# A two-layer graph-attention kernel on one core: the start of step 0, the rows of flags of step 1, the guard and the code behind it are moved

## The chip, the core and the metric

The kernel runs on one core of a Trainium2 chip. The core has five engines that run their own instruction streams: TensorE (PE, with its weight loads shown as PEld), VectorE (DVE), ScalarE (ACT), GpSimd (POOL) and SyncE (SP). An engine takes its instructions in order; one that needs another engine's result waits for a semaphore. The metric is the time of one execution on the device in microseconds (us). Before the change, three runs gave 3081.44, 3081.27 and 3081.38 us (median 3081.38).

## The reference

There are 64 graphs of 256 nodes with 512 features. Two layers of masked attention run over each graph; all is float32.

```python
def _layernorm(x): return (x - mean(x)) / sqrt(var(x) + 1e-5)

# layer 0: 4 heads of 64, keys masked by adj
h = maximum(_layernorm(x), 0)
sim = where(adj, (h @ Wq) (h @ Wk)^T / 8, -max_float)      # per head
x = x + softmax(sim) (h @ Wv) @ Wo + bo
# layer 1: 8 heads of 64, keys masked by adj | eye
h = maximum(_layernorm(x), 0)
g = _layernorm(h) * gamma + beta
scores = where(adj | eye, q k^T / 8, -1e9)                 # q, k, v = split(g @ w_qkv.T)
x = x + softmax(scores) v @ w_out.T + b_out
```

A row of `adj` without any edge makes the first softmax uniform. The kernel handles this by a flag per row: `any_of` is the maximum of a row of `adj`, and q and the mask are multiplied by the flag.

## The kernel before

**Two paths.** `fast_path` (L317) computes the softmax without subtracting a maximum, which holds as long as no sum of exponentials leaves a range. It collects the largest sums and inverse sums in `extremes`. When it has ended, a guard (L1486 to L1494) reduces `extremes` to one number, compares it with a limit and loads the answer into a register of every engine. At L1495 every engine branches: with the answer "safe" it jumps over the code of `general_path` (L25), which would compute everything again with a maximum, to the common end. With the inputs of this case the jump is always taken; the general path is never run, but its code lies between the branch and the end on every engine.

**Steps.** The fast path takes the graphs in 32 steps of two. A projection of a step is seven products of half-size blocks (`SET`, a Strassen-like scheme), which is why lines such as L898 (q and k), L945 and L979 (values) and L995 (output) come in sets of seven with evacuations from PSUM between them. The first and last steps and layer 0 of steps 0 and 1 have forms of their own.

**The order of the work is written out by hand.** `at(period, place, function)` puts each piece at a place on a common line of time; the pieces are sorted by place and issued in that order, so the place decides the order on PE, DVE, ACT and POOL (not the moment). DMA issues of SP follow the same list. Several pieces have their own place for step 0 and step 1.

**Names that the change and the prediction touch.**

- `norm0` (L662): statistics of one tile t of 128 rows (DVE, L643 and L644), variance plus epsilon (DVE, L672), its power -1/2 (POOL, L673). `first_scale` (L681): the negative mean times it (`mr`, DVE, L684), then the scaling of the tile (ACT, L685). Step 0 has four tiles: t = 0, 1 are graph 0, t = 2, 3 are graph 1.
- `first_turn` (L787) transposes a tile by PE (L794); `first_fill` (L798) copies a graph's transposed tiles with a ReLU from PSUM to `hT`, two channel blocks by ACT (L805) and two by DVE (L803). `first_qk` (L808) is a projection of q and k of one graph and one half (PE, L816), evacuated by DVE (L823) and ACT (L824).
- `neighbours` (L579) computes `any_of` by DVE (L585). `neighbours_rows` (L604) spreads the flags into a 128 x 128 tile each (`rows`, L608), by POOL for step 0 and by DVE for step 1. `neighbours_turn` (L610) turns them by PE (L614) and ACT copies them to `ne` (L619). `adjacency_transpose` turns the adjacency by PE (L551).
- The softmax sums: `key_halves` (POOL, L1086), `turn_keys` (DVE, L1092), `key_quarters` (DVE, L1099), `turn_sums` (DVE, L1152), `key_sums` (DVE, L1160 to L1164). `mask_scores` is DVE L1074, `exponentials` ACT L1079.
- `weight_block` turns the last weight matrix by PE (L496) and copies it by ACT (L498). Its four calls lie between the products of step 1's projection.
- PSUM has four banks for products, which `mm_tile` hands out in turn; a product waits until the bank's last reader has finished.
- At the end, `combine` runs the last seven products (PE, L995), and `accumulate` adds each to the result (DVE, L853 to L866). `store_block` stores the four blocks of the output (L1009, L1012). `hint_end` (L1443) loads a zero into a register and tells an engine where the branch will go, for PE and for DVE.

Of the kernel before, what the change touches and what calls it, by code (L numbers as in the profile page):

```python
# [8 lines left out]
FP = mybir.dt.float32  # L9
# [3 lines left out]
AF = mybir.ActivationFunctionType  # L13
# [11 lines left out]
def general_path(  # L25
# [18 lines left out]
    P = 128  # L44
    B, N, D = x.shape
    DH = 64
    G = 2
    NIC = N // P
    NT = G * NIC
    T = G * N  # L50
# [88 lines left out]
    def transposed(h, name, evacuate):  # L139
        hT = act.tile([P, NC, T], FP, name=name)  # L140
        for c in range(NC):
            ph = ps_mm.tile([P, T], FP, name="mm")
            for t in range(NT):
                nc.tensor.transpose(ph[:, t * P:(t + 1) * P], h[:, t, c * P:(c + 1) * P], ident)
            evacuate(hT[:, c, :], ph, c)
        return hT

    def project(hT, w, inner, lyr):

        pairs = inner // P  # L150
        qT = act.tile([P, pairs, T], FP, name=f"qT{lyr}")
        kT = act.tile([P, pairs, T], FP, name=f"kT{lyr}")
        v = act.tile([P, NT, inner], FP, name=f"v{lyr}")
        for pr in range(pairs):
            for k, dst in ((0, qT), (1, kT)):
                pp = ps_mm.tile([P, T], FP, name="mm")
                for c in range(NC):
                    nc.tensor.matmul(
                        pp, w(c, k)[:, pr * P:(pr + 1) * P], hT[:, c, :],
                        start=(c == 0), stop=(c == NC - 1),  # L160
                    )
                nc.scalar.copy(dst[:, pr, :], pp)
        for t in range(NT):
            pv = ps_mm.tile([P, T], FP, name="mm")
            for c in range(NC):
                nc.tensor.matmul(
                    pv[:, :inner], hT[:, c, t * P:(t + 1) * P], w(c, 2),
                    start=(c == 0), stop=(c == NC - 1),
                )
            nc.scalar.copy(v[:, t, :], pv[:, :inner])  # L170
        return qT, kT, v

    def probs(qT, kT, neg, g, pr):

        sc = [ps_sc.tile([P, NIC, N], FP, name="sc") for _ in range(2)]
        for ic in range(NIC):
            for e in range(2):
                rows = slice(e * DH, (e + 1) * DH)
                i0 = g * N + ic * P
                nc.tensor.matmul(  # L180
                    sc[e][:, ic, :], qT[rows, pr, i0:i0 + P], kT[rows, pr, g * N:(g + 1) * N],
                    start=True, stop=True,
                )
        pm = sm.tile([P, 2, NIC, N], FP, name="pm")
        st = stat.tile([P, 3, 2, NIC], FP, name="st")
        for e in range(2):
            for ic in range(NIC):

                nc.vector.tensor_tensor_reduce(
                    out=pm[:, e, ic, :], in0=sc[e][:, ic, :], in1=neg[:, g * NIC + ic, :],  # L190
                    scale=-SCALE, scalar=SMAX, op0=ALU.add, op1=ALU.min,
                    accum_out=st[:, 0, e, ic:ic + 1],
                )
                nc.scalar.activation(
                    pm[:, e, ic, :], pm[:, e, ic, :], AF.Exp,
                    bias=st[:, 0, e, ic:ic + 1], scale=-1.0,
                    accum_out=st[:, 1, e, ic:ic + 1],
                )
            nc.vector.reciprocal(st[:, 2, e, :], st[:, 1, e, :])
            for ic in range(NIC):  # L200
                nc.vector.tensor_scalar(
                    pm[:, e, ic, :], pm[:, e, ic, :], st[:, 2, e, ic:ic + 1], None, op0=ALU.mult
                )
        return pm

    def weigh(pm, v, oT, g, pr):

        pT = sm.tile([P, 2, NIC, N], FP, name="pT")
        for e in range(2):
            pp = ps_pt.tile([P, NIC, N], FP, name="pt")  # L210
            for jc in range(NIC):
                for ic in range(NIC):
                    nc.tensor.transpose(
                        pp[:, jc, ic * P:(ic + 1) * P], pm[:, e, ic, jc * P:(jc + 1) * P], ident
                    )
            nc.vector.tensor_copy(pT[:, e], pp)
        po = ps_mm.tile([P, T], FP, name="mm")
# [22 lines left out]

    def combine(oT, w, pairs, res):
        for t in range(NT):
            po = ps_mm.tile([P, T], FP, name="mm")
# [74 lines left out]
def fast_path(  # L318
# [14 lines left out]
    out: bass.AP,  # L333
    ident: bass.AP,
    extremes: bass.AP,
    likely: bass.AP,
):

    nc = tc.nc
# [264 lines left out]
    def neighbours_rows(s):  # L604
        rows = S[s]["rows"] = sm.tile([P, NT, P], BF, name="rows", tag="u", bufs=1)
        for t in range(NT):
            eng = nc.gpsimd if s == 0 else nc.vector
            eng.tensor_scalar(rows[:, t, :], identb, 0.0, S[s]["any"][:, t:t + 1], op0=ALU.mult, op1=ALU.add)  # L608

    def neighbours_turn(s):  # L610
        rows = S[s].pop("rows")
# [596 lines left out]
    def at(period, place, fn, *args):  # L1208
        events.append((period * (PERIOD if period >= 0 else FIRST) + place, len(events), fn, args))
# [93 lines left out]
    for s in range(NSTEP):  # L1303
# [10 lines left out]
        else:  # L1314
            at(p - 1, 4.9, adjacency_pack, s)
        for t in range(NT):
            at(p, (0.5 + 0.4 * t, (1.6995, 1.6996, 2.0295, 2.0296)[t], -6.3 + 0.01 * t)[s] if s < 3 else (0.95, 1.05, 1.2, 1.35)[t], norm0, s, t)
            if s == 0:
                at(p, 0.95 + 0.4 * t, first_scale, t)
            else:  # L1320
                at(p, (2.375 + 0.001 * t, (-5.8, -5.799, -5.6, -5.599)[t])[s - 1] if s < 3 else 1.6 + 0.001 * t, scale_row, s, t)
            if not by_tensor(s, 0):
                at(p, AT_X - 0.00035 + 0.00001 * t if s > 2 else (2.6, 2.601, 2.72, 2.721)[t], turn_blocks, s, 0, t)
        if not by_tensor(s, 0):
            at(p, AT_X - 0.00031 if s > 2 else 3.0, move_blocks, s)
        for g in range(G):
            if s < 3:
                at(p, (1.8, 2.7, -5.8)[s] + 0.001 * g, neighbours, s, g)
            else:
                at(p - 1, AT_Q0 - 0.0009, neighbours, s, g)  # L1330
        if s < 2:
            at(p, (2.9, 2.72)[s], neighbours_rows, s)
            at(p, (3.45, 3.59)[s], neighbours_turn, s)
        else:
            at(p, -4.99 if s == 2 else 0.05, neighbours_line, s)
            at(p, -4.98 if s == 2 else 0.051, neighbours_spread, s)
# [97 lines left out]


    at(NSTEP - 2, LAST_QK + 4.1 + 2 / 7, lambda: hint_end(mybir.EngineType.PE))
    at(NSTEP - 2, LAST_QK + 4.1 + 5 / 7, lambda: hint_end(mybir.EngineType.DVE))
    at(NSTEP - 2, LAST_QK + 3.5, nc.vector.memset, likely, 0)
    at(NSTEP - 3, 5.0, lambda: nc.sync.dma_start(
        wo0[:, 2], wo[:HP0 * P, HD:].rearrange("(c p) o -> p c o", p=P)  # L1440
    ))
# [28 lines left out]
        at(0, 3.61, weight_sum, nc.gpsimd, wv0, i)  # L1470
    for _, _, fn, args in sorted(events, key=lambda e: e[:2]):
        fn(*args)


def kernel(tc, *args):
# [3 lines left out]
    with tc.tile_pool(name="guard", bufs=1) as guard:  # L1479
# [4 lines left out]
        likely, safe = flags[:, 0:1], flags[:, 1:2]  # L1484
        fast_path(tc, *args, ident, extremes, likely)
        with tc.tile_pool(name="gps", bufs=1, space=bass.MemoryType.PSUM) as ps:  # L1486
            top = guard.tile([P, 1], FP, name="top")
            nc.vector.tensor_reduce(top, extremes, axis=mybir.AxisListType.X, op=ALU.max)
            row = ps.tile([1, P], FP, name="row")
            nc.tensor.transpose(row, top, ident)  # L1490
            all_top = guard.tile([1, 1], FP, name="all_top")
            nc.vector.tensor_reduce(all_top, row, axis=mybir.AxisListType.X, op=ALU.max)
            nc.vector.tensor_scalar(safe, all_top, LIMIT, None, op0=ALU.is_le)
        flag = nc.values_load(safe[0:1, 0:1], min_val=0, max_val=1, skip_runtime_bounds_check_because="a comparison gives 0 or 1")  # L1494
        with tc.If(flag < 1, label="unsafe"):  # L1495
            general_path(tc, *args)

# [28 lines left out]
```

## Time and profile before

The profiled execution took 3081.3 us, of which the span from the first to the last instruction is 3079.4 us; the median of the runs is 3081.38.

| engine | busy, us | share of the span |
|---|---|---|
| PE (matmul) | 3066.3 | 100% |
| DVE | 2537.3 | 82% |
| POOL | 2293.3 | 74% |
| ACT | 1209.6 | 39% |

The stretches at the start, by the busy time of each engine and the granted TensorE clock (1.00 is full speed):

| stretch, us | PE busy | DVE busy | ACT busy | POOL busy | PE clock |
|---|---|---|---|---|---|
| 0 to 10.8 | 6.79 | 5.09 | 3.32 | 3.04 | 0.99 |
| 10.8 to 17.4 | 6.58 | 2.52 | 2.62 | 2.38 | 0.76 |
| 17.4 to 28 | 10.60 | 4.47 | 4.41 | 5.88 | 1.00 |
| 28 to 38 | 10.00 | 7.76 | 6.81 | 7.77 | 1.00 |
| 38 to 46 | 8.00 | 7.86 | 2.53 | 5.02 | 1.00 |
| 46 to 55 | 6.20 | 8.29 | 5.22 | 6.53 | 0.81 |
| 55 to 60 | 5.00 | 4.44 | 3.56 | 3.53 | 1.00 |
| 60 to 66.6 | 6.60 | 4.57 | 3.45 | 6.28 | 1.00 |
| 100 to 200 | 100.00 | 85.96 | 40.61 | 84.41 | 1.00 |

A row's PE busy time beside its length shows how long PE stood still in it. A clock below 1.00 shows that for a part of the stretch the matmuls ran at half rate: they are "busy" but take twice as long. Times of instructions below are from the start of the span.

### The profile page before, as it was taken

To read this page: it belongs to the slowest core of one execution; us is meant where nothing else is said; L and a number is where in the kernel's file an instruction comes from. 1 tells how busy PE (TensorE), PEld (TensorE's weight loads), DVE (VectorE), ACT (ScalarE), POOL (GpSimd) and SP (SyncE) were. 2 spreads that over 40 slices of the span, in tenths; PEclk is the share of its full clock that TensorE was granted. 3 is DMA by queue.
4 is the path that set the end of the run, shared out by engine and by line. 5 is a ranking of instruction groups with operands and counts; after the bars stand their busy time and mean duration, and the time that the engine had idled before them with its cause. 6 is when DMAs were issued, how large, how long until landed. Compare 5 with 4: busy or idle time off the path is not lost.

```text
span 3079.4 us, 55409 instructions
## 1 busy us (share of the span) xinstructions
PE 3066.3 (100%) x20106; PEld 2529.9 (82%) x20106; DVE 2537.3 (82%) x4743; ACT 1209.6 (39%) x2129; POOL 2293.3 (74%) x2120
## 2 busy tenths in 40 slices
PE   9999999999999999999999999999999999999999
PEld 7888888888888888888888888888888888888887
DVE  7888888888888888888888888888888888888766
ACT  4434343334434343433434333443434344343431
POOL 6877777777877778777777777787777877778753
PEclk9999999999999999999999999999999999999999
DMA  6133132332222332223313233232232222332311
GB/s 156 52 96 94 55 94 74 89 94 76 76 82 77 94 93 62 85 73 99 94 53 93 73 92 94 66 84 74 88 94 81 73 84 74 100 89 57 92 35 50
DMA packets 192366, 251.21 MB, mean 82 GB/s; under 512 B 58264, under 2 KB 84504, under 8 KB 192088
## 3 DMA queue, kind: packets, MB, share of 16 engines
q1 hardware_dynamic: 128800, 180.46, 21.4%
q10 hardware_dynamic: 63288, 67.15, 7.6%
q8 instruction: 161, 2.64, 0.4%
q14 instruction: 117, 0.96, 0.1%
HBM read 128.59 MB, written 34.34 MB: 53 GB/s over the span
## 4 chain that ended last, share of the span: by engine, by line
PE 99%; DVE 1%; ACT 0%; DMA 0%; POOL 0%; issue 0%; SPq 0%
PE mm L898 38%; PE mm L995 18%; PE mm L979 13%; PE sc L1051 9%; PE mm L945 6%; PE sc L1122 6%; PE mm L1122 5%; PE mm L1051 3%; PE mm L816 1%; PE mm L1021 0%; PE mm L928 0%; DMA h<-in_x_dram 0%; PE mm L731 0%; DVE rows L608 0%; ACT h L659 0%; POOL pd L1086 0%
## 5 line engine op out<-in xcount | busy, mean ns | idle before, releaser
L898 PE MATMUL mm<-hT,wqkv 128*128 128x256 f32 x3584 | 787.4, 380 | 0.0
L898 PEld LDWEIGHTS mm<-hT,wqkv 128*128 128x128 f32 x3584 | 678.0, 190 | 102.5 <-issue 11.4
L1086 POOL TENSOR_TENSOR pd<-p 128x512 f32<-128x512 f32 x383 | 479.9, 1275 | 258.8 <-ACT p L1079 200.5
L995 PE MATMUL mm<-wo,oT 128*128 128x256 f32 x2632 | 578.4, 379 | 0.0
L995 PEld LDWEIGHTS mm<-wo,oT 128*128 128x128 f32 x2632 | 499.8, 190 | 68.8 <-issue 0.7
L1079 ACT ACTIVATE p<-p 128x512 f32<-128x512 f32 x766 | 441.0, 626 | 109.1 <-DVE p L1074 97.4
L1074 DVE TENSOR_TENSOR p<-sc,n 128x512 f32<-128x512 f32 x579 | 363.1, 683 | 113.3 <-PE sc L1051 113.1
L979 PE MATMUL mm<-wqkv,hT 128*128 128x256 f32 x1792 | 395.2, 381 | 0.0
L898 PE MATMUL mm<-hT,wqk 128*128 128x256 f32 x1736 | 385.0, 382 | 0.2 <-DVE qk L834 0.2
L979 PEld LDWEIGHTS mm<-wqkv,hT 128*128 128x128 f32 x1792 | 337.9, 190 | 55.0 <-issue 10.3
L898 PEld LDWEIGHTS mm<-hT,wqk 128*128 128x128 f32 x1736 | 327.7, 190 | 54.0 <-issue 10.3
L866 POOL TENSOR_TENSOR xt<-xt,u 128x512 f32<-128x512 f32 x183 | 232.7, 1272 | 140.6 <-DVE xt L860 67.5
L1051 PE MATMUL sc<-qk 64*128 64x256 f32 x2320 | 292.8, 385 | 0.0
L1051 PEld LDWEIGHTS sc<-qk 64*128 64x128 f32 x2320 | 218.0, 186 | 59.7 <-issue 27.2
L1092 DVE STREAM_TRANSPOSE turned_p<-pd 128x1024 f32<-128x1024 f32 x192 | 237.2, 1235 | 27.8 <-POOL pd L1086 27.2
L659 ACT ACTIVATE h<-h,mr,r 128x512 f32<-128x512 f32 x252 | 187.6, 804 | 170.3 <-POOL mr L655 170.3
L1198 POOL TENSOR_TENSOR oT<-oT 128x512 f32<-128x512 f32 x188 | 240.0, 1277 | 1.3 <-DMA oT<-line 1.3
L1099 DVE TENSOR_REDUCE part<-turned_p 128x32 f32<-128x1024 f32 x192 | 233.2, 1215 | 4.4
L1122 PE MATMUL sc<-p,v 128*32 128x256 f32 x3152 | 191.0, 382 | 0.0
L945 PE MATMUL mm<-hT,wv 128*128 128x256 f32 x840 | 188.3, 382 | 0.0
L851 ACT COPY u<-mm 128x512 f32<-128x512 f32 x62 | 36.3, 585 | 368.6 <-PE mm L995 215.7
L945 PEld LDWEIGHTS mm<-hT,wv 128*128 128x128 f32 x840 | 156.6, 190 | 26.8 <-ACT vT L832 6.2
(162 smaller groups left out, 4446.1 us busy)
## 6 DMA issues: line engine op xcount, KB each, us to landing
h<-blocks SPq DMA_DIRECT2D x960, 64.0 KB, 2.0
oT<-line SPq DMA_DIRECT2D x376, 128.0 KB, 3.1
h<-in_x_dram SPq DMA_DIRECT2D x31, 1024.0 KB, 5.4
xt<-in_x_dram ACTq DMA_DIRECT2D x60, 512.0 KB, 4.8
out_dram<-xt SPq DMA_DIRECT2D x32, 512.0 KB, 3.1
v<-values ACTq DMA_DIRECT2D x480, 32.0 KB, 1.9
out_dram<-xt ACTq DMA_DIRECT2D x30, 512.0 KB, 4.5
ne<-ne SPq DMA_DIRECT2D x90, 64.0 KB, 2.0
```

The source lines that it names most:

```text
L898: nc.tensor.matmul(bank[:, k, :], w[:, wa, c, k, a * P:(a + 1) * P], st["hT"][:, ba, c, :], start=first and (k, c) == (0, 0), stop=(k, c) ...
L945: nc.tensor.matmul(bank, wv0[:, wa, c, :], st["hT"][:, ba, c, :], start=first and c == 0, stop=c == HC - 1, skip_group_check=True,)
L979: nc.tensor.matmul(bank[:, t, :], st["hT"][:, ba, c, t * P:(t + 1) * P], wqkv1[:, wa, c, 2, :], start=first and (t, c) == (0, 0), stop=(t, ...
L995: nc.tensor.matmul(bank[:, t, :], oT[:, ba, c, t * P:(t + 1) * P], w[:, wa, c, :], start=first and (t, c) == (0, 0), stop=(t, c) == (NIC - ...
L1051: nc.tensor.matmul(sc[g][e][:, kc, :], qk[rows, 1, k0:k0 + P], qk[rows, 0, g * N:(g + 1) * N], start=True, stop=True,)
L1074: nc.vector.tensor_tensor(p[e][:, g], sc[e], neg[:, :, g, :], ALU.add)
L1079: nc.scalar.activation(p[e][:, g], p[e][:, g], AF.Exp, scale=SCALE)
L1086: nc.gpsimd.tensor_tensor(st["pd"][:, e], p[e][:, :, 0, :], p[e][:, :, 1, :], ALU.add)
L1092: nc.vector.transpose(st["turned_p"], st.pop("pd").rearrange("p e g (b k) -> p (e g b) k", k=32))
L1099: nc.vector.tensor_reduce(st["part", lyr, prs][:, i], st.pop("turned_p"), axis=mybir.AxisListType.X, op=ALU.add)
L1122: nc.tensor.matmul(po[r0:r0 + 32, g, :], (st["v1"][:, g * NIC + kc, pr * P + r0:pr * P + r0 + Q] if lyr else st["v0"][:, r0 // Q, pr, g * ...
L1198: nc.gpsimd.tensor_tensor(dst, dst, invb, ALU.mult)
```

## The change

It has four parts.

1. **Step 0, tiles 2 and 3.** `norm0` of t = 2, 3 moves from places 1.3 and 1.7 to 1.73 and 1.74, behind `first_fill` of graph 0 (1.72); `first_scale` of t = 2 from 1.75 to 1.745; that of t = 0, 1 and 3 stays. On DVE the statistics of tiles 2 and 3 so stand behind `mr` of tile 1 and the two fills of graph 0.
2. **Step 1, flags.** `neighbours` of step 1 moves from place 2.7 to 2.03, on DVE in front of the last evacuation of q of step 0 (L823). `neighbours_rows` of step 1 is done by ACT (four activations with the flag as bias and a scale of zero) in place of DVE, and moves from 2.72 to 2.9297, behind the first copy of attention output (L1137).
3. **Guard.** The three DVE instructions and the PE transpose of the guard move into the list, among the last seven products: the first reduction behind the second product's evacuation, the transpose behind the fourth product, the last reduction and the comparison behind the fourth product's evacuation, and the load of the flag into the registers in front of the last evacuation. The transpose takes one of the four product banks. The hint for DVE is removed, that for PE stays.
4. **General path.** It loops over 64 single graphs in place of 32 pairs (G = 1), and some of its DVE work goes to ACT. It isn't run, but its code gets shorter: from the branch to the end, DVE has 139 instructions in place of 298, ACT 137 in place of 144.

```diff
@@ general_path
-    G = 2
+    G = 1
...
-            nc.vector.reciprocal(st[:, 2, e, :], st[:, 1, e, :])
+        nc.vector.reciprocal(st[:, 2], st[:, 1])
+        for e in range(2):
             for ic in range(NIC):
-                nc.vector.tensor_scalar(
-                    pm[:, e, ic, :], pm[:, e, ic, :], st[:, 2, e, ic:ic + 1], None, op0=ALU.mult
+                nc.scalar.activation(
+                    pm[:, e, ic, :], pm[:, e, ic, :], AF.Copy, scale=st[:, 2, e, ic:ic + 1]
                 )
...
-            nc.vector.tensor_copy(pT[:, e], pp)
+            nc.scalar.copy(pT[:, e], pp)
@@ fast_path
         for t in range(NT):
-            eng = nc.gpsimd if s == 0 else nc.vector
-            eng.tensor_scalar(rows[:, t, :], identb, 0.0, S[s]["any"][:, t:t + 1], op0=ALU.mult, op1=ALU.add)
+            if s == 0:
+                nc.gpsimd.tensor_scalar(rows[:, t, :], identb, 0.0, S[s]["any"][:, t:t + 1], op0=ALU.mult, op1=ALU.add)
+            else:
+                nc.scalar.activation(rows[:, t, :], identb, AF.Identity, bias=S[s]["any"][:, t:t + 1], scale=0.0)
...
-            at(p, (0.5 + 0.4 * t, (1.6995, ...)[t], ...)[s] ..., norm0, s, t)
+            at(p, ((0.5, 0.9, 1.73, 1.74)[t], (1.6995, ...)[t], ...)[s] ..., norm0, s, t)
             if s == 0:
-                at(p, 0.95 + 0.4 * t, first_scale, t)
+                at(p, (0.95, 1.35, 1.745, 2.15)[t], first_scale, t)
...
-                at(p, (1.8, 2.7, -5.8)[s] + 0.001 * g, neighbours, s, g)
+                at(p, (1.8, 2.03, -5.8)[s] + 0.001 * g, neighbours, s, g)
...
-            at(p, (2.9, 2.72)[s], neighbours_rows, s)
+            at(p, (2.9, 2.9297)[s], neighbours_rows, s)
...
-    at(NSTEP - 2, LAST_QK + 4.1 + 5 / 7, lambda: hint_end(mybir.EngineType.DVE))
+    likely, safe = flags[:, 0:1], flags[:, 1:2]
     at(NSTEP - 2, LAST_QK + 3.5, nc.vector.memset, likely, 0)
+    at(NSTEP - 2, LAST_QK + 4.1 + 2.5 / 7, lambda: guard_top())
+    at(NSTEP - 2, LAST_QK + 4.1 + 3.5 / 7, lambda: guard_row())
+    at(NSTEP - 2, LAST_QK + 4.1 + 4.5 / 7, lambda: guard_safe())
+    at(NSTEP - 2, LAST_QK + 4.1 + 6.5 / 7, lambda: G_OF.update(flag=nc.values_load(safe[0:1, 0:1], ...)))
+    def guard_top():
+        G_OF["top"] = guard.tile([P, 1], FP, name="top")
+        nc.vector.tensor_reduce(G_OF["top"], extremes, axis=mybir.AxisListType.X, op=ALU.max)
+    def guard_row():
+        G_OF["row"] = mm_tile([1, P])
+        nc.tensor.transpose(G_OF["row"], G_OF["top"], ident)
+    def guard_safe():
+        all_top = guard.tile([1, 1], FP, name="all_top")
+        nc.vector.tensor_reduce(all_top, G_OF["row"], axis=mybir.AxisListType.X, op=ALU.max)
+        nc.vector.tensor_scalar(safe, all_top, LIMIT, None, op0=ALU.is_le)
@@ tile_gnn_kernel
-        fast_path(tc, *args, ident, extremes, likely)
...
+        flag = fast_path(tc, *args, ident, extremes, flags, guard)
         with tc.If(flag < 1, label="unsafe"):
             general_path(tc, *args)
```

More of the change, by code (lines that the diff above doesn't have):

```diff
@@ L141, in transposed @@
         for c in range(NC):
-            ph = ps_mm.tile([P, T], FP, name="mm")
+            ph = ps_mm.tile([P, D], FP, name="mm")
             for t in range(NT):
                 nc.tensor.transpose(ph[:, t * P:(t + 1) * P], h[:, t, c * P:(c + 1) * P], ident)
-            evacuate(hT[:, c, :], ph, c)
+            evacuate(hT[:, c, :], ph[:, :T], c)
         return hT
@@ L155, in project @@
             for k, dst in ((0, qT), (1, kT)):
-                pp = ps_mm.tile([P, T], FP, name="mm")
+                pp = ps_mm.tile([P, D], FP, name="mm")
                 for c in range(NC):
                     nc.tensor.matmul(
-                        pp, w(c, k)[:, pr * P:(pr + 1) * P], hT[:, c, :],
+                        pp[:, :T], w(c, k)[:, pr * P:(pr + 1) * P], hT[:, c, :],
                         start=(c == 0), stop=(c == NC - 1),
                     )
-                nc.scalar.copy(dst[:, pr, :], pp)
+                nc.scalar.copy(dst[:, pr, :], pp[:, :T])
         for t in range(NT):
-            pv = ps_mm.tile([P, T], FP, name="mm")
+            pv = ps_mm.tile([P, D], FP, name="mm")
             for c in range(NC):
@@ L215, in weigh @@
                     )
-            nc.vector.tensor_copy(pT[:, e], pp)
-        po = ps_mm.tile([P, T], FP, name="mm")
+            nc.scalar.copy(pT[:, e], pp)
+        po = ps_mm.tile([P, D], FP, name="mm")
         for jc in range(NIC):
@@ L242, in combine @@
         for t in range(NT):
-            po = ps_mm.tile([P, T], FP, name="mm")
+            po = ps_mm.tile([P, D], FP, name="mm")
             for pr in range(pairs):
@@ L335, in fast_path @@
     extremes: bass.AP,
-    likely: bass.AP,
+    flags: bass.AP,
+    guard,
 ):
@@ L1316, in fast_path @@
         for t in range(NT):
-            at(p, (0.5 + 0.4 * t, (1.6995, 1.6996, 2.0295, 2.0296)[t], -6.3 + 0.01 * t)[s] if s < 3 else (0.95, 1.05, 1.2, 1.35)[t], norm0, s, t)
+            at(p, ((0.5, 0.9, 1.73, 1.74)[t], (1.6995, 1.6996, 2.0295, 2.0296)[t], -6.3 + 0.01 * t)[s] if s < 3 else (0.95, 1.05, 1.2, 1.35)[t], norm0, s, t)
             if s == 0:
-                at(p, 0.95 + 0.4 * t, first_scale, t)
+                at(p, (0.95, 1.35, 1.745, 2.15)[t], first_scale, t)
             else:
@@ L1436, in fast_path @@
     at(NSTEP - 2, LAST_QK + 4.1 + 2 / 7, lambda: hint_end(mybir.EngineType.PE))
-    at(NSTEP - 2, LAST_QK + 4.1 + 5 / 7, lambda: hint_end(mybir.EngineType.DVE))
+    likely, safe = flags[:, 0:1], flags[:, 1:2]
     at(NSTEP - 2, LAST_QK + 3.5, nc.vector.memset, likely, 0)
+    at(NSTEP - 2, LAST_QK + 4.1 + 2.5 / 7, lambda: guard_top())
+    at(NSTEP - 2, LAST_QK + 4.1 + 3.5 / 7, lambda: guard_row())
+    at(NSTEP - 2, LAST_QK + 4.1 + 4.5 / 7, lambda: guard_safe())
+    at(NSTEP - 2, LAST_QK + 4.1 + 6.5 / 7, lambda: G_OF.update(flag=nc.values_load(
+        safe[0:1, 0:1], min_val=0, max_val=1, skip_runtime_bounds_check_because="a comparison gives 0 or 1"
+    )))
+    G_OF = {}
+    def guard_top():
[8 more added lines that the diff above has]
+        nc.vector.tensor_scalar(safe, all_top, LIMIT, None, op0=ALU.is_le)
     at(NSTEP - 3, 5.0, lambda: nc.sync.dma_start(
@@ L1472, in fast_path @@
         fn(*args)
+    return G_OF["flag"]
 def kernel(tc, *args):
@@ L1483 @@
         flags = guard.tile([1, 2], I32, name="flags")
-        likely, safe = flags[:, 0:1], flags[:, 1:2]
-        fast_path(tc, *args, ident, extremes, likely)
[L1486 to L1494, printed above, removed]
+        flag = fast_path(tc, *args, ident, extremes, flags, guard)
         with tc.If(flag < 1, label="unsafe"):
```

## The prediction

> **What bounds the kernel.** PE is busy 3066.3 of the 3079.4 us span, so time can only be won where PE stands still or runs slowly. The table of stretches says where: nothing between 100 and 200 us, but 4.0 us of idle time before 10.8, 2.8 us between 46 and 55, and a clock of 0.76 and 0.81 in two stretches. What follows the last matmul is the third place. First I read the chain of work that ended last, here for the first 11 us (start, length, what):
>
> ```profile
> 3.23 4.64 DMA h<-in_x_dram
> 7.87 0.02 issue
> 7.89 0.70 DVE bs L643
> ...
> 8.82 0.02 issue
> 8.84 0.15 DVE ve L672
> 8.99 0.13 DVE mr L684
> 9.13 0.03 issue
> 9.15 0.82 ACT h L685
> 9.97 0.04 issue
> 10.02 0.34 PE sc L794
> ```
>
> The DMA that lands at 7.87 is tile 2. But `mr` at 8.99 belongs to tile 1: its variance was ready at 5.60 (L672, 5.45 + 0.15) and its power on POOL at 6.25. DVE, in order, sat behind tile 2's statistics. PE waited 2.5 us for graph 0 because graph 1 was late.
>
> The timeline shows the second place (PE, ACT, DVE in turn; in brackets the idle time before and who ended it):
>
> ```profile
> 46.87 0.61 PE L551 MATMUL mm<-identb,both 128*128 128x128 bf16 x8
> 50.06 0.66 PE L496 MATMUL mm<-ident,wr 128*128 128x128 f32 x4 [2.58 <-ACT wo L498]
> 50.94 3.29 PE L898 MATMUL mm<-hT,wqk 128*128 128x256 f32 x8 [0.22 <-DVE qk L834]
> ...
> 46.56 2.42 ACT L1079 ACTIVATE p<-p 128x512 f32<-128x512 f32 x4 [4.89 <-DVE p L1074]
> ...
> 38.72 1.27 DVE L585 TENSOR_REDUCE any_of<-ad 128x2 f32<-128x512 uint8 x2
> 39.91 3.06 DVE L608 TENSOR_SCALAR rows<-identb,any_of 128x128 bf16<-128x128 bf16 x4
> 42.89 0.83 DVE L1152 STREAM_TRANSPOSE keys<-part 32x32 f32<-32x32 f32 x4
> ```
>
> PE's L496 needs a bank that ACT frees (L498); ACT has that copy queued behind four exponentials, these wait 4.89 us for DVE, and DVE was at step 1's flags.
>
> The end, in the waits of SP's queue:
>
> ```profile
> SPq L1521 <- DVEq L1495: 1.9, 1, 1.9
> ```
>
> SP gathers the end and waits 1.94 us for DVE. By the instructions of line 1495, the five branches run from 3074.8 to 3074.9; POOL, ACT and PE execute their next instruction at 3075.3 to 3075.4, DVE at 3078.41, 3.50 us after its branch ended. No matmul or store is in that gap.
>
> **Part 1, tiles 2 and 3.** Nothing is added, only the order changes. With durations from the trace: `mr` of tile 1 at 6.45 (POOL's power ends at 6.25, and for tile 0 `mr` came 0.20 after it), ACT scales 6.69 to 7.50 (0.81), PE turns from 7.55, fills by ACT from 7.92 and by DVE 8.03 to 8.79, L816 from 8.36 instead of 10.82. Its weights landed at 5.79 and 6.72. What is late next is graph 1. DVE takes tile 2 at 8.70 (landed, but the fills are first) instead of 7.89; statistics, variance, tile 3: the two variances end at 9.80 and 10.81, POOL's powers at 10.43 and 11.44, then POOL's cast of the adjacency (1.04) to 12.46 and its four `rows` (0.37 each) to 13.87, against 13.52 before. ACT scales tile 3 at 12.28 to 13.09. PE runs L816 x16 at 0.216 each until 11.82, turns tiles 2 and 3 by 13.58 with 0.9 us of gap, turns `rows` by 13.97 and the adjacency by 14.42. Then the 48 matmuls of L816 start, at 14.42 against 17.44: **-3.0 us**. The moved flags of graph pair 0 stay near 11 us, so SP's next load, which reuses their input, isn't later than its 12.63.
>
> Here rule and row differ. The matmuls from 10.82 took 0.427 us each and those after 13.94 0.216: the granted clock was 0.5 for one stretch of 3.41 us after the first wait, and for another (51.48 to 54.90) after the second. "TensorE: Matmul & The Clock Gate" of the Trainium skill (section "What's actually happening") says that the gate falls to half after at least one idle window of about 3.4 us. Neither wait is that long (2.5 and 2.6 us), so by the rule the clock would not be part of the sum; by the row each wait also costs about 1.6 us of slow matmuls. I take the row: the -3.0 holds 1.8 us of it.
>
> **Part 2, flags of step 1.** The two `any_of` (1.27) move to the gap of 1.42 us in which DVE waits for PE's last L816 (28.06). Shifted by -3.0, that gap lies at 23.6 to 25.0, so they just fit. They need the adjacency of step 1; its DMA was issued at 12.63, and its neighbours on the queue landed at 18.60 and 21.07. If it lands after 23.7, the rest is late one for one. The four `rows` leave DVE. On ACT no row shows this operation; ACT took 0.20 for 128x1 (L700) and 0.37 for 128x256 (L824), so 0.8 to 1.5 us for four; I take 1.1, near the middle. They start at 38.0 behind L1137 in a gap of 4.89 us in front of the exponentials. If the gap closes to 0, they cost their 1.1.
>
> So DVE goes from L1099 straight to L1152: -1.27 -3.06 +0.1 = -4.2, with the -3.0 about -7.2. But the next product of DVE, L1074, needs PE's scores: 30.94 came 1.26 after L1051's start, and 40.94 shifted is 37.9, so 39.2 against 45.89, -6.7. Exponentials end at 42.3, the first L498 at 43.4. PE reaches L496 (after L551) at 44.4: no wait. L834 needs the product that ends at 43.8, and DVE is free at 43.6: it ends at 44.6, PE's L898 goes at 44.85. The next bank is free at 46.2, PE is there at 46.6. From the end of L551 (47.32) to the second round of L1122 (54.96) PE needed 7.64 us for 4 + 8 + 4 matmuls and a first round; at full speed these are 0.44 + 1.83 + 0.25 + 0.37 = 2.9: **-4.75 us**, of it 2.8 of waits. What comes next late? POOL's normalisation L1198 at 63.47 to 64.74, needed by L1021 at 66.64; its inputs (sums of unit 1, statistics of step 2) move by 7 to 8 us with the rest, so the 1.9 us of slack stay. Behind 66.6 PE never waits, so the gain is kept whole.
>
> **Part 3, guard.** The transpose enters PE's stream in front of the fifth of the last seven products. Nearest rows: L794, same shape, 0.109 a piece; L995 beside it 0.216: bounds 0.1 and 0.25, I take **+0.11**. The bank it takes pushes the fifth product to the bank that L857 frees at 3066.9; PE is there at 3067.7. On DVE 0.27 + 0.14 + gaps = 0.5 us come in front of L855 (3069.87), where three additions follow without a gap; the last waits 1.02 us for PE, so 0.5 of that cover remains. ACT's load of the flag (0.57) lies between its last two stores, which stood 1.8 us apart. The guard's own chain (3073.7 to 3074.8) was never what ended last: SP waited until 3075.59 for the landing of ACT's last store, 1.78 us after L860's end. It buys nothing.
>
> **Part 4, shorter code.** The trace lists fetches of instructions: 117 packets of 8 KB for the 14,400 instructions of the four engines other than PE, so some 125 per packet. ACT jumped over 144 instructions (less the 6 at the end) without a stall (0.44 us to its next instruction), DVE over 298 with one. DVE's jump of 139 is now within what ACT's row shows. DVE crosses into a new packet about 28 instructions before its branch, ACT 32: both land in the next one, already there. Bounds 0.44 (ACT) and 3.5 (no help); I take 0.44. The rule here: "Runtime: NRT & Kernel Launch" of the Trainium skill (section "Instruction fetch mechanics") has blocks of 16 KiB and a window of two, some 512 instructions; by it DVE's 298 would have been inside and its 3.5 us would have another cause, and shortening gains nothing (0). The 8 KB packets contradict it; I take the row. The removed hint took no fetch with it: after PE's hint at 3064.0 a 16 KB packet follows at 3065.0, after DVE's at 3071.2 none until 3075.9. With DVE in time, SP's waits run on: each of them takes 0.07, and the 1.94 becomes 0.06: **-1.88**.
>
> **Sum.** -3.0 - 4.75 + 0.11 - 1.88 = -9.5. From the profiled run's 3081.3 (span 3079.4 and 1.9 around it; 0.1 below the median) this gives 3071.8, a span of 3069.9. Change outside +-0.2% (6.2 us, about what a measurement of this kernel tells from none) is called faster or slower.
>
> **Rivals.**
> - *The clock falls anyway* (0.15): PE still has gaps of about 1.3 us in 12 to 14 us. For: a wait of 2.5 us sufficed. Against: half that. One slow stretch costs 1.7: 3073.5.
> - *DVE's jump still misses* (0.11): the window is known from ACT alone. 1.88 is not won: 3073.7.
> - *The second wait only moves* (0.13): margins on L834 and L498 are 0.2 to 0.4 us, and POOL is 79% busy from 46 to 66.6 (16.3 of 20.6 us). Then 3.0 + 1.8 is won: 3076.6, no change by the bound.
> - *Slower: the adjacency of step 1 lands late* (0.03). The trace proves only that POOL's cast had it at 32.55. At 32.5, `any_of` ends at 33.8, L823 5.7 later than before; of this DVE's 4.2 come back, PE idles long enough for one more slow stretch: +1.5 + 1.7 - 1.8 = +1.4, 3082.7. It decides from a landing of about 31 us on. Against it: the queue's neighbours landed by 21.07.
>
> **Chances.** My forecast has 0.58. Bounds of the unknown costs (rows, transpose, margins) are +-1.0, and gaps of PE that I left in could close: likeliest range 3070.5 to 3073.0. With the first two rivals and most of what lies between them and the third, the range is 3069.8 to 3075.2. Faster by over 0.2%: 0.84; within: 0.13; slower: 0.03.
>
> **What would show it.** L816's first matmul at 8.4 and its 48 from 14.4; no clock of 0.5 before 3000; L496 in the product set without a wait for L498; L1021 near 58.9; the last L860 at 3065.4; DVE's next instruction half a microsecond after its branch, and SP's last landing, not DVE, ending the waits. I am wrong if PE's idle time turns up elsewhere before 59 us, behind `rows` on POOL or ACT, or if the flags on DVE hold L823.

## The result

Before and after were run in turn on one chip, nine runs each. Before: median 3081.38 us (3079.84 to 3082.52). After: **3072.65 us** (3072.26 to 3073.46). The ratio is 0.9973 (95% interval 0.9962 to 0.9983), a gain of 8.7 us or 0.28%. The forecast was 3071.8, range 3069.8 to 3075.2. The gain lies above the 0.2% that the prediction set as the bound, so "faster" came true, though not by much: the interval reaches down to 0.17%. The profiled execution has a span of 3070.9 us (forecast 3069.9), before 3079.4.

**The profile after.** PE is still the bound:

```profile
PE 3063.4 (100%) x20106; PEld 2527.4 (82%) x20106; DVE 2534.3 (83%) x4739; ACT 1212.2 (39%) x2133; POOL 2295.8 (75%) x2120
```

The timeline of the first 62 us after (start, length, engine, line, operation; in brackets the idle time before and who ended it). Three to four lines were inserted above these pieces, so L816 of before is now L820, L496 is L498, L498 is L500, L1074 is L1078 and L1021 is L1025:

```profile
8.22 3.72 PE L820 MATMUL mm<-hT,wqk 128*128 128x256 f32 x16
12.99 0.66 PE L798 MATMUL sc<-ident,h 128*128 128x128 f32 x4 [0.62 <-ACT h L689]
14.31 10.58 PE L820 MATMUL mm<-hT,wqk 128*128 128x256 f32 x48
23.43 1.25 DVE L587 TENSOR_REDUCE any_of<-ad 128x2 f32<-128x512 uint8 x2
24.93 0.42 DVE L827 TENSOR_TENSOR qk<-mm,ne 128x256 f32<-128x256 f32 x1 [0.26 <-PE mm L820]
38.43 1.28 ACT L612 ACTIVATE rows<-identb,any_of 128x128 bf16<-128x128 bf16 x4
38.98 2.48 DVE L1078 TENSOR_TENSOR p<-sc,n 128x512 f32<-128x512 f32 x4 [0.19 <-PE sc L1055]
44.18 0.61 PE L498 MATMUL mm<-ident,wr 128*128 128x128 f32 x4
44.76 1.99 PE L902 MATMUL mm<-hT,wqk 128*128 128x256 f32 x8
```

The 16 matmuls of L820 take 3.72 us where they took 5.24, so they run at full clock. The 48 start at 14.31 (before 17.44, -3.13). The flags fill DVE's gap and leave 0.26 us of it. The four `rows` take ACT 1.28 us. L498 at 44.18 has no bracket: the wait of 2.58 us is gone. L1025 starts at 58.84, 7.80 us earlier than before.

At the end SP's waits no longer close with DVE coming late from its branch; they close with the landing of the stores:

```profile
SPq L1016 <- DVEq L1511: 1.9, 1, 1.9
SPq L1511 <- SPq L1511: 1.9, 1, 1.9
```

L1511 is the branch: the first line is SP waiting, before its last store, for the last evacuation (DVE's branch comes right behind it); the second is the landing.

The sum of the change, from the two traces:

| stretch | before, us | after, us | difference |
|---|---|---|---|
| start to the first L1021 / L1025 | 66.64 | 58.84 | -7.80 |
| from there to the end of the last evacuation | 3007.16 | 3007.54 | +0.38 |
| last evacuation to the landing of the last store | 1.79 | 2.57 | +0.78 |
| landing to the end of the span | 3.84 | 1.93 | -1.91 |
| span | 3079.43 | 3070.88 | -8.55 |

The head did what was forecast (-7.75). The last row has the size that was forecast for part 4 (-1.88); which part makes it is tested below. The third row is new: the last store lands 0.78 us later behind its evacuation, which the forecast didn't have.

### The profile page after: what moved, and what is told of

Its sections match the earlier page's. It is cut to its first block, busy times and chain, and to the rows that moved or that the text cites. A ratio compares the mean times of both kernels' runs of the same rounds, so it can differ in the third digit from the quotient of the medians.

```text
span 3070.9 us, 55407 instructions
## 1 busy us (share of the span) xinstructions
PE 3063.4 (100%) x20106; PEld 2527.4 (82%) x20106; DVE 2534.3 (83%) x4739; ACT 1212.2 (39%) x2133; POOL 2295.8 (75%) x2120
## 4 chain that ended last, share of the span: by engine, by line
PE 100%; DVE 0%; issue 0%; ACT 0%; POOL 0%; POOLq 0%
PE mm L902 38%; PE mm L999 19%; PE mm L983 13%; PE sc L1055 9%; PE sc L1126 6%; PE mm L949 6%; PE mm L1126 5%; PE mm L1055 3%; PE mm L932 1%; PE mm L1025 0%; PE mm L820 0%; PE mm L789 0%; PE mm L735 0%; PE mm L498 0%; PE sc L798 0%; PE mm L553 0%
## 5 line engine op out<-in xcount | busy, mean ns | idle before, releaser
L1078 DVE TENSOR_TENSOR p<-sc,n 128x512 f32<-128x512 f32 x579 | 363.1, 683 | 113.1 <-PE sc L1055 113.1
```

Source lines behind the costliest of these rows:

```text
L1078: nc.vector.tensor_tensor(p[e][:, g], sc[e], neg[:, :, g, :], ALU.add)
```

## The experiments

### The end: guard, code and landing

The question was what took back 0.8 us. Theory: the guard among the last evacuations is harmful. Rival: it is the shorter code, or the chip, that delays the landing. Three kernels and the changed one again ran on one chip; part 3 alone and the kernel without the hint ran on another.

**Parts 1, 2 and 4, with the guard put back to its old place** (it takes the guard out of the list of pieces and back behind `fast_path`):

```diff
@@ of the changed kernel
-    at(NSTEP - 2, LAST_QK + 4.1 + 2.5 / 7, lambda: guard_top())
-    at(NSTEP - 2, LAST_QK + 4.1 + 3.5 / 7, lambda: guard_row())
-    at(NSTEP - 2, LAST_QK + 4.1 + 4.5 / 7, lambda: guard_safe())
...
-        flag = fast_path(tc, *args, ident, extremes, flags, guard)
+        fast_path(tc, *args, ident, extremes, flags, guard)
...
+            nc.vector.tensor_reduce(top, extremes, axis=mybir.AxisListType.X, op=ALU.max)
+            nc.tensor.transpose(row, top, ident)
...
+        flag = nc.values_load(safe[0:1, 0:1], ...)
```

> The changed kernel with the guard back behind the last evacuation (parts 1, 2 and 4 stay). Theory A, the early branches let the engines fetch instructions while the last stores run, and one of the DMA engines falls behind: the last store then lands 1.8 us after the last evacuation (2.57 us in the changed kernel, 1.78 us in the one before), the transpose leaves PE's stream (0.11), and the span is about 3070.0 against 3070.9. Theory B, the late landing of the changed kernel was chance: it differs from run to run, and the span is 3070.9 to 3071.0. Theory C, the early guard does shorten the end: the span grows by up to 1 us, 3071.9.

Measured: 3071.71 us (3071.27 to 3072.45, 7 runs), ratio to before 0.997 (0.9959 to 0.9981); span 3069.5, landing 1.80 us after the last evacuation.

**The changed kernel again**, beside it:

> The changed kernel itself, beside the others on the same chip. Theory A: a span of 3070.9 +- 0.2 and a last store that lands 2.4 to 2.6 us after the last evacuation. Theory B: the landing differs by 0.5 us or more from the first profile.

Measured: 3072.78 us (3072.29 to 3073.57, 8 runs), ratio 0.9973 (0.9963 to 0.9984); span 3071.3, landing 3.24 us. The ranges of the two kernels overlap by 0.2 us; the medians differ by 1.07.

**Parts 1 to 3 with the old, long code** (the changed kernel with `general_path` of before):

```diff
@@ of the changed kernel, general_path
-    G = 1
+    G = 2
```

(and the rest of the diff of `general_path` undone)

> The changed kernel with the old, long general path (parts 1, 2 and 3; the hint for DVE stays removed). As the prediction had it, the shorter code alone is worth 1.88 us: DVE's next instruction comes 3.5 us after its branch and the span is about 3072.7. Theory D, formed from the trace after the change: DVE's branch is now at 3065.6, ahead of the last evacuation, so a fetch of 3.5 us ends at 3069.2, before SP asks for DVE at 3069.9; the span stays at 3070.9, and parts 3 and 4 are two ways to the same gain.

Measured: 3072.86 us (one run), span 3071.0. DVE's queue still takes 2.94 us from its branch (3065.31) to the next instruction behind it (3068.25). But it branches so early that the store lands only at 3069.05, and SP asks at 3069.06: DVE's stall lies beside the stores and costs nothing.

**Part 4 alone** (`general_path` of after in the kernel before, the hint for DVE removed):

> The kernel before with part 4 alone (single graphs in the general path, hint for DVE removed; guard at the end as before). Packets of 8 KB and a window that reaches into the next one: DVE's next instruction comes 0.5 us after its branch in place of 3.5, SP's 1.94 us wait is gone, and the span is 3077.5 (-1.9). Rival, a window of some 512 instructions, so that the 3.5 us have another cause: 3079.4.

Measured: 3080.04 us (one run), span 3078.2. The next instruction of DVE's queue comes 0.58 us after the start of its branch (before 3.59), and from the last evacuation to the end it is 3.72 us in place of 5.63: -1.91. (The rival's window is that of the page which the prediction cites for the fetches.) That the span is only 1.3 us shorter comes from ahead of the end: the first L1021 is 0.46 us later (see the clock below), and from there to the last evacuation it takes 0.20 us longer.

**Part 3 alone** (the guard as in after, the long code and the hint kept):

> The kernel before with part 3 alone (guard among the last products; long general path, hint for DVE kept). By the prediction part 3 buys nothing and costs 0.11. Theory D: DVE's fetch of 3.5 us now runs behind the last evacuation and the stores, so SP does not wait for DVE; the stores land 2.5 to 3.3 us after the last evacuation; from the last evacuation's end to the end of the span 4.5 to 5.2 us, against 5.63 before.

Measured: 3080.61 us (one run), span 3078.8; from the last evacuation to the end 5.10 us (-0.53), landing 3.17 us.

**The hint alone**: is it the missing hint, not the length, that changes DVE's jump?

```diff
@@ of the kernel before
-    at(NSTEP - 2, LAST_QK + 4.1 + 5 / 7, lambda: hint_end(mybir.EngineType.DVE))
```

> The kernel before without the hint for DVE, and nothing else. Theory: the hint fetched nothing (no packet follows it); DVE's next instruction comes 3.5 us after its branch, and from the last evacuation's end to the end of the span it takes 5.6 us, as before. Rival, the hint had started the fetch: with it gone DVE comes later and the end takes 6 us or more.

Measured: 3079.47 us (one run), span 3077.6. It is 1.8 us shorter than the profiled span of before (3079.4) for a reason at the other end: its second wait in the first 60 us was not followed by half clock (table of the clock below). The instructions of the branch's line (L1494 in this kernel, one line less) in the kernel without the hint; the columns are the shortest, median and longest duration, then first and last start:

```profile
L1494 DVEq COMPARE_BRANCH  x1: 72/72/72, 3073.0 to 3073.0; - x1
...
L1494 PEldq EVENT_SEMAPHORE  x1: 51/51/51, 3073.4 to 3073.4; - x1
L1494 DVEq EVENT_SEMAPHORE  x1: 21/21/21, 3076.6 to 3076.6; - x1
```

and the same in the kernel with part 4 alone (L1495):

```profile
L1495 DVEq COMPARE_BRANCH  x1: 72/72/72, 3075.5 to 3075.5; - x1
...
L1495 PEldq EVENT_SEMAPHORE  x1: 51/51/51, 3076.0 to 3076.0; - x1
L1495 DVEq EVENT_SEMAPHORE  x1: 21/21/21, 3076.1 to 3076.1; - x1
```

Without the hint DVE comes 3.6 us after its branch, as with it: the hint did nothing. With the shorter code it comes 0.6 us after, close to PE's 0.5: the length of the jump decides. That the limit comes from packets of 8 KB, as the prediction took it, is not shown: the runs have only 298 instructions, with a stall, and 139, without. In before, the three packets of 8 KB behind the branch start at 3075.88 to 3075.95 and are through by 3076.5, and DVE goes on 1.9 us later, so the fetches in sight don't fill its stall.

The end in eight of the kernels:

| kernel | guard | code | landing after the last evacuation, us | end after it, us |
|---|---|---|---|---|
| before | last | long | 1.79 | 5.63 |
| no hint | last | long | 1.80 | 5.67 |
| part 4 | last | short | 1.79 | 3.72 |
| parts 1, 2, 4 | last | short | 1.80 | 3.73 |
| part 3 | early | long | 3.17 | 5.10 |
| parts 1 to 3 | early | long | 3.00 | 4.93 |
| after | early | short | 2.57 | 4.50 |
| after, again | early | short | 3.24 | 5.17 |

Two things stand out. First, in the last six rows the end is the landing plus 1.93 us; only where the guard is last and the code long does DVE's stall come on top. So parts 3 and 4 are two ways to take DVE's stall off the end: one moves DVE's branch away from the end, the other makes it short. Second, the landing takes 1.78 to 1.80 us in all ten traces with the guard last (those of the next sections included), and 2.57 to 3.24 us in all four with it early. The place of the guard decides it; code length doesn't. Nor are the last stores issued later: in all 14 traces SP issues its last one 0.30 us before the end of the last evacuation and ACT 0.03 us after it.

Why does a guard delay a store? The view of the DMAs gives a reading, taken from the issue of the fourth store before the end to the last landing. After (4.9 us):

```profile
## 3 DMA queue, kind: packets, MB, share of 16 engines
q1 hardware_dynamic: 416, 0.39, 25.1%
q10 hardware_dynamic: 416, 0.39, 23.4%
q14 instruction: 3, 0.02, 1.6%
q8 instruction: 1, 0.02, 1.4%
issues: line engine op xcount, KB each, median us to landing
out_dram<-wqk SPq DMA_DIRECT2D x1, 256.0 KB, 3.5
...
out_dram<-wqk SPq DMA_DIRECT2D x1, 128.0 KB, 2.6
```

Parts 1, 2 and 4 with the guard last (4.2 us, the same four stores):

```profile
q1 hardware_dynamic: 416, 0.39, 28.5%
q10 hardware_dynamic: 416, 0.39, 27.5%
issues: line engine op xcount, KB each, median us to landing
out_dram<-wqk SPq DMA_DIRECT2D x1, 256.0 KB, 2.2
...
out_dram<-wqk SPq DMA_DIRECT2D x1, 128.0 KB, 1.7
```

The same 832 packets of data, but after has four packets of instructions among them, and a store of 256 KB takes 3.5 us in place of 2.2. With the guard early an engine branches as soon as its own work is done: POOL at 3063.4, PE at 3063.9, DVE at 3065.6, while the last stores are under way. Fetches of instructions follow: PE's 16 KB from 3065.11 for 1.12 us, 8 KB packets at 3064.45, 3067.19 and 3067.97. The trace has sixteen reports for each store, and the store has landed with the last of them. Of the first of these stores the second-last report comes at 3066.31 and the last at 3067.68, 1.37 us behind; in the other three kernels with the guard early that lag is 1.79, 1.98 and 2.06 us, and with the guard last it is 0.01 to 0.02 us in all ten. Of the last store, fourteen reports have come by 3068.16, the last two at 3068.93 and 3068.95. So one or two of the sixteen are late, and the fetches are the only other packets in the view. With the guard last all four fetches come at 3067.9 to 3068.0, after the landing at 3067.6. That the guard's place delays the landing is shown by these 14 traces; that it does so through these packets is read from their times and not varied by itself.

### The head: tiles, flags and the clock

Each of the two parts alone, and part 2 in halves, on one chip.

**Part 1 alone**:

```diff
@@ of the kernel before
-            at(p, (0.5 + 0.4 * t, ...)[s] ..., norm0, s, t)
+            at(p, ((0.5, 0.9, 1.73, 1.74)[t], ...)[s] ..., norm0, s, t)
...
-                at(p, 0.95 + 0.4 * t, first_scale, t)
+                at(p, (0.95, 1.35, 1.745, 2.15)[t], first_scale, t)
```

> The kernel before with part 1 alone (tiles 2 and 3 of step 0 behind graph 0's fills). Theory: the 48 matmuls of L816 start 3.0 us earlier, the wait of 2.58 us at L496 and one stretch of half clock near 48 us stay, and the 3.0 us are kept to the end: span 3076.4. Rival, the gain is lost at the second wait, which gets longer: L1021 starts at 66.6 as before, span 3079.4.

Measured: 3076.26 us (one run), span 3074.5. The 48 matmuls start at 14.29, as in after. But the first L1021 comes at 61.85, 4.79 us earlier, not 3.1: the wait at L496 is still there (2.56 us), and yet the clock doesn't fall behind it.

**Part 2 alone**:

```diff
@@ of the kernel before
-                at(p, (1.8, 2.7, -5.8)[s] + 0.001 * g, neighbours, s, g)
+                at(p, (1.8, 2.03, -5.8)[s] + 0.001 * g, neighbours, s, g)
...
-            at(p, (2.9, 2.72)[s], neighbours_rows, s)
+            at(p, (2.9, 2.9297)[s], neighbours_rows, s)
```

(and the `rows` by ACT)

> The kernel before with part 2 alone (both: any_of of step 1 earlier, rows by ACT). Theory: first wait and first half-clock stretch stay; no wait at L496, no second half-clock stretch, L1021 4.75 us earlier, span 3074.7. Rival, any_of holds L823 at 28 us: the gain is smaller by what L823 is later.

Measured: 3077.81 us (one run), span 3076.0. From the 48 to L1021 it takes 44.53 us, as in after (before 49.20, -4.67). But the 48 start at 18.83, 1.39 later than before, although nothing ahead of them was changed: the clock is at half for two stretches of 3.41 us.

**The rows alone** (ACT and place 2.9297, `neighbours` left at 2.7):

> The kernel before with the rows of step 1 by ACT alone (any_of stays at its old place). DVE reaches L1074 3.06 us earlier, at 42.8; the exponentials end at 45.9, L498 at 46.9, PE wants its bank at 47.3. Theory: no wait there, at most 0.3 us at L898; gain 4.4 to 4.75, span 3074.7 to 3075.0. Rival, both halves of part 2 are needed: a wait of over 1 us stays and the gain is under 3.5.

Measured: 3076.38 us (one run); 48 to L1021 44.60 us, no wait at L496. The rows alone bring 4.60 of the 4.67. From the 48, L1076 (L1074 of before) starts 0.79 us later than in after (25.46 against 24.67 us), and PE loses only 0.07 of it.

**The flags alone** (place 2.03, rows left on DVE):

> The kernel before with any_of of step 1 moved alone (rows stay on DVE). DVE reaches L1074 1.27 us earlier, at 44.6, and PE still waits at L496 for 1.3 us and 0.2 at L898. If a wait this short keeps the clock: gain 1.3 + 1.6 = 2.9, span 3076.5. If half a window of idle time is enough for half clock: gain 1.3, span 3078.1. By the rule that it takes an idle window of 3.4 us there was no clock to win in the first place, and the gain is 1.3 with a clock of 1.0.

Measured: 3077.46 us (one run); 48 to L1021 45.16 us, so the flags alone bring 4.04 of the 4.67. The wait at L496 is 0.15, and 0.23 at the L898 behind it. Only 1.27 us left DVE there, but the wait shrank by 2.4. The rows got cheaper by being earlier: the `rows` of this kernel (durations shortest, median, longest in ns):

```profile
L608 DVE TENSOR_SCALAR rows<-identb,any_of x4: 243/247/1342, 39.1 to 40.7; 128x128 bf16<-128x128 bf16 x4
```

and of the kernel before:

```profile
L608 DVE TENSOR_SCALAR rows<-identb,any_of x4: 242/874/1308, 39.9 to 41.7; 128x128 bf16<-128x128 bf16 x4
```

One of four is long where two were (and a third took 0.47). See the last section. Behind a wait of 0.15 us there was no half clock either, so the gain is above all three that were expected. (The rule named there is that of the page which the prediction cites for the clock.)

**The clock, in all these runs.** Every change of the clock within one trace lies a multiple of 3.413 us from every other (before: 10.523 and 51.483 are 12 x 3.413 apart), so the clock is decided on a fixed grid of such windows. Laid on that grid, the wait of 2.6 us at L496 falls differently from run to run. The table of stretches, one row for each window, in the kernel with part 4 alone (L496 is L497 there, its wait is 2.58 us; columns: length, then busy time of PE, PEld, DVE, ACT, POOL, granted clock, DMA):

```profile
45.43:48.85 3.42, 2.51 (x20) 2.04 (x17) 3.42 (x7) 1.83 (x4) 0.00 (x0) 1.00 0.57 199
48.85:52.26 3.41, 1.52 (x8) 1.21 (x9) 2.84 (x4) 3.08 (x7) 3.34 (x3) 1.00 0.92 270
52.26:55.67 3.41, 3.41 (x22) 2.10 (x24) 3.27 (x7) 0.59 (x1) 3.41 (x4) 0.50 0.76 264
```

and in part 1 alone (wait 2.56 us):

```profile
42.06:45.47 3.41, 2.27 (x17) 1.80 (x16) 3.41 (x7) 2.08 (x4) 0.18 (x1) 1.00 0.65 196
45.47:48.88 3.41, 1.77 (x9) 1.43 (x10) 2.85 (x4) 2.83 (x7) 3.41 (x3) 1.00 1.02 314
48.88:52.29 3.41, 3.41 (x46) 2.18 (x45) 3.23 (x8) 0.96 (x2) 3.41 (x4) 1.00 0.67 223
```

The same wait, split 0.91 + 1.89 us of idle PE in the one and 1.14 + 1.64 in the other. After a window with 1.89 us of idle the clock is 0.50 and the next window holds 22 matmuls; after 1.64 it is 1.00 and the window holds 46. The windows in which the two waits of before lie, in all traces that keep one or both and show the clock there:

| kernel | wait | idle of PE in the windows, us | clock of the window after the last |
|---|---|---|---|
| part 3 | second | 1.52, 1.26 | 1.00 |
| no hint | second | 1.23, 1.57 | 1.00 |
| part 1 | second | 1.14, 1.64 | 1.00 |
| part 4 | second | 0.91, 1.89 | 0.50 |
| no hint | first | 2.08 | 0.50 |
| before | second | 0.59, 2.21 | 0.50 |
| part 3 | first | 2.21 | 0.50, and again 0.50 |
| part 2 | first | 2.26 | 0.50, and again 0.50 |
| rows | first | 2.34 | 0.50 |
| before | first | 2.52 | 0.50 |
| part 4 | first | 1.44, 2.57 | 0.50 |
| flags | first | 2.97 | 0.50 |

In a window of 3.413 us at full clock, the limit behind which the clock falls lies between 1.64 and 1.89 us of idle; no row contradicts it. Where it stayed low for a second window, the first one at half clock had 0.88 and 0.92 us of idle of its own; where it rose again, at most 0.27. So a wait of 2.5 us may cost nothing, one window (up to 1.7 us) or two, by where it lies on the grid. The kernel after has no window with more than 0.62 us of idle from 7 us to its last products, and so nothing to lose here: its 17 runs lie within 1.3 us (3072.26 to 3073.57), the 36 of before in four groups within 3.4 us (3079.24 to 3082.59). That the clock makes this spread is likely, not shown. For 27 of the 36 the mean clock is on record, to 0.001: the 11 with 0.999 have a median of 3080.98 us, the 16 with 0.998 one of 3081.53, and their ranges overlap.

### A better kernel, and one step more

**Parts 1, 2 and 4 again, and with the flags of step 0 earlier.** In after, PE waits 0.62 us at 12.99 for tile 3. The second kernel moves the flags of graph pair 0 and the cast of its adjacency ahead of tiles 2 and 3:

```diff
@@ of the kernel with parts 1, 2, 4
-            at(p, (2.0, 2.4, -5.95)[s], adjacency_cast, s)
+            at(p, (1.71, 2.4, -5.95)[s], adjacency_cast, s)
...
-                at(p, (1.8, 2.03, -5.8)[s] + 0.001 * g, neighbours, s, g)
+                at(p, ((1.715, 1.8)[g] if s == 0 else (2.03, -5.8)[s - 1] + 0.001 * g), neighbours, s, g)
```

> The kernel with the guard last once more, beside the other. Theory A (fetches and stores collide in the changed kernel): its last store again lands 1.8 us after the last evacuation, and the time is 1 us below the changed kernel's 3072.65 to 3072.78. If the landing is now 2.5 us or more, theory A falls.

> The guard at the end, and two more moves in step 0: the first any_of of step 0 (graph 0) goes into DVE's idle time in front of the fills (6.5 to 7.9), and POOL's cast of the adjacency into POOL's idle time from 6.3 on. Theory: what holds the 48 matmuls of L816 at 14.3 is POOL's cast and rows behind two powers and tile 3 behind both any_of; with both gone they start at 13.5 to 13.6, and the gain is kept: span 0.7 to 0.8 below that of the kernel with the guard last, 3068.8. Rival, the any_of (0.68) delays the fills and so everything by as much as it saves: no change. In time this is 0.02%, less than a comparison of times can show; the trace decides.

Measured, on one chip: parts 1, 2 and 4 3071.43 us (3071.3 to 3072.41, 6 runs), ratio 0.9968 (0.9956 to 0.9981); with the flags moved 3070.99 us (3070.52 to 3075.89, 7 runs), ratio 0.9969 (0.9958 to 0.998). The two can't be told apart. The 48 matmuls do start 0.6 us earlier (13.70), but L1025 comes at 59.44, later than the 58.87 of the other: PE has a new wait at 55.4. Its timeline:

```profile
46.90 4.97 POOL L537 TENSOR_TENSOR xt<-xt,bo_b 128x512 f32<-128x512 f32 x4 [2.94 <-PE mm L618]
53.06 2.28 POOL L632 TENSOR_TENSOR n<-n,ne 128x512 bf16<-128x512 bf16 x2
55.41 1.97 PE L902 MATMUL mm<-hT,wqk 128*128 128x256 f32 x8 [0.98 <-POOL n L632]
```

POOL's additions to `xt` start at 46.90 here and at 45.54 in the first profile of parts 1, 2 and 4. They need `xt` from DRAM: issued at 37.98 and landing 8.8 us later (46.8), against 37.78 and 7.6 us (45.4). The bracket names PE, but the landing is what came just before. The head moved up, the loads didn't: SP's four issues of weights ahead of `xt` took 3.56 us in place of 1.92, and these weights landed after 9.8 us in place of 7.8. In this trace the loads are what limits the first 60 us next.

How far that holds for other executions is open. The loads vary by themselves: in the second profile of parts 1, 2 and 4, the same kernel, `xt` lands 5.9 us after its issue, not 7.6, and POOL's additions start at 44.55. And the execution profiled here was one of the slower ones (3072.03 us; of the others one took 3072.01 and one 3075.89). The remaining four took 3070.52 to 3070.99 us, 0.4 to 0.9 below the 3071.43 of the other kernel, which is what 0.6 us kept to the end would give; none of them was profiled.

## Why the prediction held, and where it was off

**Part 1 (-3.0): held, -3.13.** The L820 start at 8.22 (forecast 8.4) and the 48 at 14.31 (14.42). That PE waits for tile 3 for a while was in the sum as 0.9 us of gap; 0.6 came.

**Part 2 (-4.75): held, -4.67.** 48 to L1021 49.20 to 44.53. The rows on ACT took 1.28 (taken: 1.1 of 0.8 to 1.5), the two `any_of` 1.25 in the gap of 1.42. What the sum didn't see is that either half alone brings most of it, the rows 4.60 and the flags 4.04: the sum priced the two as if DVE's time came off one for one, but a part of it was enough to end the wait and the half clock behind it. With the rows off DVE, the flags could have stayed (44.60 against 44.53). And of the 4.67 about 1.6 is the half clock of one profile: with part 1 alone, where that clock stayed full, the stretch takes 47.56 us, which leaves 3.03 for part 2.

**Clock: the right size, the wrong certainty.** The prediction weighed the page's "at least one idle window" against the row and took the row: "each wait also costs about 1.6 us of slow matmuls". For the profiled run of before that held, and with it the sum. But it isn't a cost of the wait: with part 1 alone a wait of 2.56 us costs none, and with part 2 alone the first wait costs two windows. Of the five traces that keep the second wait, three have no half clock behind it, so that the profile of before had one behind each wait was in part luck. The page ("TensorE: Matmul & The Clock Gate" of the Trainium skill, section "What's actually happening") also says that the window is free-running, and this explains it once a window counts as idle with more than about half of it idle (between 1.64 and 1.89 of 3.41 us at full clock here), not all of it. The rival "the clock falls anyway" was priced with gaps of 1.3 us: by this table they couldn't have done it.

**Part 3 (+0.11, "it buys nothing"): this is the step that failed.** The transpose cost its 0.11 us. But the argument stopped at the guard's own chain. An early flag also lets the engines branch early, and then their fetches fall among the last stores: the landing after the last evacuation was taken at its old 1.78 us and measured 2.57 (3.24 in the second profile). Nor does it buy nothing everywhere: alone, with the long code behind it, it took 0.53 us off the end.

**Part 4 (-1.88): held for what it names.** DVE's next instruction comes 0.58 us after the start of its branch in part 4 alone, and the end shrinks by 1.91. (Two readings of the prediction were loose. The gap behind DVE's branch is not free of stores: the last one lands in it, at 3075.59. And in the window of two blocks from the page that it cites, a target 298 instructions ahead lies inside only where the branch stands early enough in its block, so the miss alone doesn't contradict that page; the packets of 8 KB do.) With the guard early, part 4 adds nothing: parts 1 to 3 with the long code have the same 1.93 us behind the landing. In after the same term is 5.63 - 4.50 = 1.13, because 0.78 goes to the landing. That is the mis-sized term of the whole sum; another 0.3 us of the 1.0 between -9.5 and -8.55 lies in +0.38 in place of +0.11 between L1025 and the last evacuation. The traces split it. The last seven products take 12.35 to 12.36 us in the ten traces with the guard last and 12.46 to 12.47 in the four with it early: that is the transpose, at its 0.11. The other 0.27 lies ahead of these products, where the guard has no part: from L1021 to their start it takes 2993.83 to 2994.28 us in the 14 traces, 2994.01 in before and 2994.28 in after. Its cause stays open.

**Rivals.** None of the four decided. "DVE's jump still misses" named the end as the weak place, and the loss was there, from the landing and not the jump; with the guard early the missed jump would have cost nothing (parts 1 to 3 with the long code: 3072.86). The second wait didn't move, and the adjacency of step 1 was there at 23.43.

**What the kernel should have.** Parts 1, 2 and 4 without 3: medians of 3071.71 and 3071.43 us in two groups of runs, 1.07 us below the changed kernel where both ran on one chip.

## What to carry to other kernels

When the work ahead of a kernel's last branch is moved away from the end, ask what the engines do once they are let go: here their fetches fell among the last stores, and the last landing is on the path. Before pricing a wait by the slow matmuls behind it, lay it on the grid of the clock's windows: how much of one window it leaves idle decided in these traces, and a profile shows one position of it. And when two edits are made at one place, run each alone: of parts 3 and 4 one was enough, and of part 2 either half brought most.

## What the runs showed of the hardware

- **The clock's windows**, as in the table: a fixed grid of 3.413 us; a window at full clock with 1.89 us or more of idle PE is followed by half clock, with 1.64 or less by full.
- **Instruction fetches beside stores**: 40 KB of fetches (16 + 3 x 8) within the last 5 us of after go with a landing of its last store 0.8 us later, 1.4 us in its second profile.
- **A DVE instruction can be held for the length of one of POOL's.** Of the four `rows` in before, the third takes 1.28 us and ends at 41.74, POOL's addition ends at 41.69; the fourth 1.31 us, to 42.97, POOL's to 42.92. Where only one addition overlaps (flags alone) one of them is long, 39.40 to 40.74, POOL's to 40.69. Each ends 0.05 us after POOL's, and so does the first of before, of 0.47 us (40.38, POOL's 40.33). The two `any_of`, beside the same POOL instruction, keep their 0.68. The page "SBUF — State Buffer" of the Trainium skill (section "SBUF: two separate sides") has a port pair that POOL shares with some of DVE's instructions; the one that starts first holds it for its whole length, and the other blocks. These numbers agree with it for `rows`. By this reading it is why two of four `rows` cost 1.3 us, and why moving them to ACT (0.39 to 0.41 each) freed 3.06 us of DVE and not four times 0.24. No run here takes POOL's addition away to test it.
